# Layer 3's gelu written out over ACT, GpSimd and VectorE, with its down projections two pairs behind

## The chip, the cores and the metric

The kernel runs on one NeuronCore of a Trainium2 chip. The metric is device time in microseconds, the median over executions. Five engines work side by side, each through its own queue of instructions in order: TensorE (PE, with its weight loads shown apart as PEld), VectorE (DVE), ScalarE (ACT), GpSimd (POOL) and SyncE (SP, which issues DMAs here).

## What is computed

Four layers of cross-attention and feed-forward on 2048 tokens of width 256 with a context of 1601 tokens, all in float32, each with a layer norm ahead and a residual. The change is in the last feed-forward block, layer 3, which gives each of eight experts 256 consecutive tokens:

```python
def _L3_ffn_ref(x, w1, b1, w2, b2):
    E = w1.shape[0]                      # 8 experts, width 256, hidden 1024
    tokens = x.reshape(E, T, D)          # T = 256
    h = jnp.einsum('etd,edf->etf', tokens, w1) + b1[:, None, :]
    h = jax.nn.gelu(h)                   # the tanh form
    y = jnp.einsum('etf,efd->etd', h, w2) + b2[:, None, :]
    return y.reshape(B, S, D)
```

The tanh form of gelu is 0.5 h (1 + tanh(0.79788 (h + 0.044715 h^3))).

## The kernel before

Layer 3 is one function, layer3_tail, in which attention and feed-forward are woven together. Tokens come in four chunks of 512 (c = 0 to 3), heads in four groups of four (g), so there are 16 units u = (c, g). Keys come in four tiles of 100 (TK), the part of the context that the mask can close; so the main loop has 64 steps n = (u, kt). The order on TensorE is that of the program text (a manual schedule for PE); on the other engines a scheduler lays the order down when the program is built, and each engine follows it.

One step of the main loop does, in this order: scores of tile kt (L1584, eight matmul records into two psc buffers) and their exponentials on ACT (L1591, two of 100x1024); values of the step before (L1601); maxima of a later unit, first half (L1566 on PE, reduced by VectorE, L1570); one feed-forward bit; the second half of the maxima; a projection of queries (L1551, its two copies qb and q by ACT, L1555 and L1556), or a shift, or a normalisation (L1615, L1617), and, when a chunk is finished, an output projection (L1634); another bit; up to two reciprocals. The psc pool has two buffers, so the maxima of a step wait for its exponentials to have read the scores, and the next scores wait for VectorE's reductions. After a chunk's last head group GpSimd multiplies attention by the reciprocals (L1626).

A bit is one entry of the list that feed_forward(c) makes when the chunk's attention is done; feed(n) runs the next n of them. A chunk has 35 bits: begin (a norm), then for each of its two experts eight steps up, eight steps down and end. With two bits a step, 64 steps do not take all 140, and the experts 5, 6 and 7 are left for the time after the main loop.

- up(e, f, k): two matmuls of 128x256 (L1665) into one half of psu, a PSUM tile of one buffer, then ACT's gelu with the bias b1, from psu into h (L1671). f counts in pairs, k is 0 or 1 within the pair.
- down(e, f, k): two matmuls (L1681) from h and w2 into psy, which sums over all eight.
- end(e): for both token tiles GpSimd adds x and b2 into y (L1691), VectorE adds psy (L1692), SP sends y out (L1693); then the weights of expert e + 2 are loaded (L1531 to L1533). y comes from the pool hp, which has two buffers.

In the list, the steps down of a pair come one pair behind its steps up: up 0, up 1, down 0, up 2, down 1, up 3, down 2, down 3, end.

Of the kernel before, what the change touches and what calls it, by code (L numbers as in the profile page):

```python
# [8 lines left out]
F32 = mybir.dt.float32  # L9
BF16 = mybir.dt.bfloat16  # L10
F32R = mybir.dt.float32r
AF = mybir.ActivationFunctionType
ALU = mybir.AluOpType
AX = mybir.AxisListType

P = 128
D = 256
# [3 lines left out]
CH = 512  # L21
# [32 lines left out]
class Net:  # L54
# [1360 lines left out]
    def layer3_tail(self, mask):  # L1415
        tc, nc, a = self.tc, self.nc, self.a
        H, DH, G = 16, 16, 4
# [4 lines left out]
        with ExitStack() as s:  # L1422
            kv = s.enter_context(tc.tile_pool(name="kv3", bufs=1))
            qp = s.enter_context(tc.tile_pool(name="q3", bufs=3))
            pp = s.enter_context(tc.tile_pool(name="p3", bufs=5))
            op = s.enter_context(tc.tile_pool(name="o3", bufs=2))
# [44 lines left out]
            with ExitStack() as s0:  # L1471
                self.banks(s0)
                for w in (wkT, wqT, wop):
                    nc.gpsimd.memset(w, 0.0)
                nc.gpsimd.memset(v, 0.0)
                nc.gpsimd.memset(v.rearrange("p k (h e) -> p (k h) e", e=32)[:, :, DH : DH + 1], 1.0)
                self.transpose_weight(wkT, raw["Wk"], pad=True)
                self.transpose_weight(wqT, raw["Wq"], pad=True)
                wvT = kv.tile([P, 2, D], F32, name="wvT")
                self.transpose_weight(wvT, raw["Wv"])  # L1480
                nc.vector.tensor_copy(
                    wop.rearrange("p o (h e) -> p (o h) e", e=32)[:, :, 0:DH],
                    raw["Wo"].rearrange("p o (h e) -> p (o h) e", e=DH),
                )
                for g in range(0, G, 2):
                    ps = self.pm()
                    for k in range(2):
                        for o in range(2):
                            nc.tensor.transpose(
                                ps[:, k * D + o * P : k * D + (o + 1) * P],  # L1490
                                wop[:, o, (g + k) * P : (g + k + 1) * P], self.ident,
                            )
                    nc.scalar.copy(woT[:, g : g + 2, :], ps.rearrange("p (k o) -> p k o", k=2))
                for g in range(G):
                    ps = self.pm()
                    for kc in range(2):
                        nc.tensor.matmul(
                            ps[:, :NTAIL], lhsT=wkT[:, kc, g * P : (g + 1) * P], rhs=self.ctxT[:, kc, K0:],
                            start=kc == 0, stop=False,
                        )  # L1500
                    nc.tensor.matmul(ps[:, :NTAIL], lhsT=to17, rhs=away, start=False, stop=True)
                    nc.scalar.activation(kT[:, g, :], ps[:, :NTAIL], AF.Identity, bias=kbias[:, g : g + 1])
                    nc.vector.tensor_copy(kb[:, g, :], kT[:, g, :])
                for kt in range(TK):
                    ps = self.pm()
                    for kc in range(2):
                        nc.tensor.matmul(
                            ps[:TR, :D], lhsT=self.ctxT[:, kc, K0 + kt * TR : K0 + (kt + 1) * TR],
                            rhs=wvT[:, kc, :], start=kc == 0, stop=kc == 1,
                        )  # L1510
                    nc.vector.tensor_tensor(
                        v[:TR, kt, :].rearrange("p (h e) -> p h e", e=32)[:, :, 0:DH],
                        ps[:TR, :D].rearrange("p (h e) -> p h e", e=DH),
                        bv[:TR].rearrange("p (h e) -> p h e", e=DH), ALU.add,
                    )
# [4 lines left out]
            hp = s.enter_context(tc.tile_pool(name="f3h", bufs=2))  # L1520
            E, NF = 8, 8
            b1r = kv.tile([E * NF, P], F32, name="b1r")
            nc.sync.dma_start(b1r, a["L3_ffn_b1"].rearrange("e (f p) -> (e f) p", p=P))
            b1 = kv.tile([P, E * NF], F32, name="b1")
            experts = {}

            def load_expert(e):
                w1 = wp.tile([P, 2, NF * P], F32, name="w1")
                w2 = wp.tile([P, NF, D], F32, name="w2")
                b2 = wp.tile([P, D], F32, name="b2")  # L1530
                nc.sync.dma_start(w1, a["L3_ffn_w1"][e].rearrange("(k p) f -> p k f", p=P))  # L1531
                nc.sync.dma_start(w2, a["L3_ffn_w2"][e].rearrange("(k p) f -> p k f", p=P))
                nc.sync.dma_start(b2, a["L3_ffn_b2"][e].partition_broadcast(P))  # L1533
                experts[e] = w1, w2, b2
# [7 lines left out]
            xnT, q, qb, p_of, acc, attn = {}, {}, {}, {}, {}, {}  # L1542
# [87 lines left out]
            def out_project(c, i):  # L1630
                x = self.x[c * TPC + i]
                ps = self.pm()
                for k in range(G):
                    nc.tensor.matmul(  # L1634
                        ps[:, :D], lhsT=attn[c][:, k, i * P : (i + 1) * P], rhs=woT[:, k, :],
                        start=k == 0, stop=k == G - 1,
                    )
                nc.gpsimd.tensor_tensor(x, x, bo, ALU.add)
                nc.vector.tensor_tensor(x, ps[:, :D], x, ALU.add)
                if i == TPC - 1:  # L1640
                    fbits.extend(feed_forward(c))
# [4 lines left out]
            def feed_forward(c):  # L1646

                state = {}

                def begin():  # L1650
                    if c == 0:
                        ps = self.pm()
                        nc.tensor.transpose(ps[:, : E * NF], b1r, self.ident[: E * NF, : E * NF])
                        nc.vector.tensor_copy(b1, ps[:, : E * NF])
                    state["x"] = self.norm(c)

                def up(e, f, k):
                    w1 = experts[e][0]
                    if k == 0:
                        if f == 0:  # L1660
                            state["h"] = hp.tile([P, NF, 256], F32, name="h3")
                        state["ps"] = psf.tile([P, 2, 256], F32, name="psu", tag="u")
                    ps = state["ps"][:, k, :]
                    for kc in range(2):
                        nc.tensor.matmul(  # L1665
                            ps, lhsT=w1[:, kc, (f + k) * P : (f + k + 1) * P],
                            rhs=state["x"][:, kc, (e % 2) * 256 : (e % 2 + 1) * 256],
                            start=kc == 0, stop=kc == 1,
                        )
                    at = e * NF + f + k  # L1670
                    nc.scalar.activation(  # L1671
                        state["h"][:, f + k, :], ps, AF.Gelu_apprx_tanh, bias=b1[:, at : at + 1]
                    )

                def down(e, f, k):
                    w2 = experts[e][1]
                    if f + k == 0:
                        state["acc"] = psf.tile([P, 2, D], F32, name="psy", tag="y")
                    acc = state["acc"]
                    for i in range(2):  # L1680
                        nc.tensor.matmul(  # L1681
                            acc[:, i, :], lhsT=state["h"][:, f + k, i * P : (i + 1) * P], rhs=w2[:, f + k, :],
                            start=f + k == 0 and i == 0, stop=f + k == NF - 1 and i == 1,
                        )

                def end(e):
                    b2 = experts.pop(e)[2]
                    for i in range(2):
                        t = 2 * e + i
                        y = hp.tile([P, D], F32, name="y")  # L1690
                        nc.gpsimd.tensor_tensor(y, self.x[t], b2, ALU.add)  # L1691
                        nc.vector.tensor_tensor(y, state["acc"][:, i, :], y, ALU.add)  # L1692
                        nc.sync.dma_start(self.out[0, t * P : (t + 1) * P, :], y)  # L1693
                    if e + 2 < E:
                        load_expert(e + 2)

                yield begin, ()
                for e in (2 * c, 2 * c + 1):
                    for f in range(0, NF + 2, 2):
                        for k in range(2):  # L1700
                            if f < NF:
                                yield up, (e, f, k)
                        for k in range(2):
                            if f:
                                yield down, (e, f - 2, k)
                    yield end, (e,)

            def feed(n):
# [17 lines left out]
            for n in range(U * TK):  # L1726
# [12 lines left out]
                elif tasks:  # L1739
                    f, args = tasks.pop(0)  # L1740
                    f(*args)
                if later:
                    f, args = later.pop(0)
# [14 lines left out]
            while later:  # L1758
                f, args = later.pop(0)
# [116 lines left out]
```

## Time and profile before

| | |
|---|---|
| median of three runs | 2328.24 us (2322.44 to 2330.52) |
| the profiled execution | 2327.4 us, span 2325.7 us, mean granted PE clock 0.924 |
| layer 3's attention steps with feed-forward bits | about 1930 to 2245 us |
| experts 5, 6, 7 after the main loop | about 2247 to 2321 us |
| ACT in 1930 to 2245 us, table loads | 51 of 1.283 us |
| GpSimd busy, 1950 to 2000 us | 3.93 us of 50 |

Times are from one execution. A line of the groups gives the source line, engine, operation and tiles, count, busy time and mean duration, then the engine's idle time just before these instructions and what ended it. A line of the waits gives who waited for whom, the total, the number of times and the longest. A line of the timeline gives start, length, engine, source line and operation, and in square brackets the idle time before it and its releaser. TensorE's times are modelled from the instructions' sizes, and a float32 matmul appears as two records. ACT_TABLE_LOAD is the instruction with which ScalarE changes the set of functions that it can evaluate.

### The profile page before, as it was taken

The numbers are of one execution on the slowest core, as the hardware profiler recorded it, in microseconds if no ns is written. First come the engines' busy times: TensorE is split into PE (matmuls) and PEld (weight loads), VectorE is DVE, ScalarE is ACT, GpSimd is POOL, SyncE is SP. The second block draws the span as 40 slices with busy tenths as digits, with TensorE's granted clock in tenths as the row PEclk, the third lists the DMA queues.
The fourth block names the chain that finished last, engine by engine and source line by source line (L and its number), as shares of the span: only waits on it lengthen the run. The fifth ranks groups of instructions, "written<-read, shape, count | busy, mean of one in ns | idle before, by whom it ended". The sixth has DMA issues, their size and how long they took to land.

```text
span 2325.7 us, 22833 instructions
## 1 busy us (share of the span) xinstructions
PE 2006.3 (86%) x8841; PEld 974.4 (42%) x8841; DVE 1208.8 (52%) x2252; ACT 781.0 (34%) x1018; POOL 631.9 (27%) x405
## 2 busy tenths in 40 slices
PE   7799999999986887898978899998877887878887
PEld 3233333333325332344436645555762223333445
DVE  4665555646434999856455532323664453444411
ACT  4544344344440100000224421111433445656441
POOL 1178778778680000000000210000340001000000
PEclk9799999999995999999978999998887788998998
DMA  8810000000000000001010000000002000111111
GB/s 286 269 43 1 1 1 1 1 1 1 1 1 0 1 0 1 0 0 64 0 38 0 21 1 1 0 1 0 1 6 77 1 3 10 34 43 43 43 62 33
DMA packets 39699, 63.51 MB, mean 27 GB/s; under 512 B 5133, under 2 KB 32158, under 8 KB 39582
## 3 DMA queue, kind: packets, MB, share of 16 engines
q1 hardware_dynamic: 37776, 60.33, 8.0%
q10 hardware_dynamic: 1806, 1.64, 0.2%
q8 instruction: 71, 1.16, 0.2%
q14 instruction: 46, 0.38, 0.1%
HBM read 59.87 MB, written 2.10 MB: 27 GB/s over the span
## 4 chain that ended last, share of the span: by engine, by line
PE 65%; DVE 19%; ACT 6%; issue 4%; DMA 3%; POOL 2%; SPq 0%; ACTq 0%; DVEq 0%; POOLq 0%
PE pa L454 6%; PE psc L442 5%; PE psc L627 5%; PE psc L766 4%; PE pa L786 4%; DVE ge L576 4%; PE psc L1584 4%; PE psu L1665 3%; DVE mp L367 3%; PE psy L1681 3%; DVE ge L578 2%; ACT p L1591 2%; DVE ri L404 2%; PE pm L1551 2%; PE pa L1601 1%
## 5 line engine op out<-in xcount | busy, mean ns | idle before, releaser
L463 POOL TENSOR_TENSOR sp<-sp,p 128x1024 f32<-128x1024 f32 (+1 forms) x176 | 418.5, 2378 | 61.6 <-ACT p L447 51.1
L367 DVE TENSOR_REDUCE mp<-pm 128x1 f32<-128x512 f32 x384 | 242.7, 680 | 160.5 <-PE pm L362 159.8
L447 ACT ACTIVATE p<-psc 128x1024 f32<-128x1024 f32 (+1 forms) x208 | 212.9, 1023 | 260.2 <-PE psc L442 169.2
L1570 DVE TENSOR_REDUCE ms<-psc 128x2 bf16<-128x800 f32 x128 | 123.7, 992 | 191.8 <-PE psc L1566 191.8
L442 PE MATMUL psc<-qT,kT 64*128 64x512 f32 (+1 forms) x832 | 221.3, 593 | 0.0
L454 PE MATMUL pa<-p,v 128*64 128x512 f32 (+1 forms) x832 | 202.8, 609 | 0.0
L593 PE MATMUL psc<-ge,pick 128*8 128x512 bf16 x512 | 142.3, 378 | 37.9 <-DVE ge L576 18.9
L1591 ACT ACTIVATE p<-psc 100x1024 f32<-100x1024 f32 x128 | 124.4, 1022 | 94.0 <-PE psc L1584 93.6
L362 PE MATMUL pm<-kb,qb 64*128 64x512 bf16 x384 | 101.8, 393 | 28.0 <-DVE mp L367 26.4
L627 PE MATMUL psc<-w_e,xe 128*128 128x512 f32 x256 | 110.4, 593 | 0.0
L1626 POOL TENSOR_TENSOR attn<-o,ri 128x512 f32<-128x512 f32 x16 | 20.2, 1264 | 328.0 <-DVE ri L1624 306.2
L454 PEld LDWEIGHTS pa<-p,v 128*64 128x64 f32 (+1 forms) x832 | 50.9, 137 | 131.2 <-issue 128.1
L1584 PE MATMUL psc<-q,kT 32*100 32x512 f32 x512 | 96.1, 732 | 10.5 <-DVE ms L1570 10.3
L135 POOL TENSOR_SCALAR rstd<-mv 128x4 f32<-128x4 f32 x32 | 10.5, 328 | 345.0 <-DVE mv L133 345.0
L766 PE MATMUL psc<-q,kT 128*128 128x512 f32 (+1 forms) x208 | 102.2, 610 | 0.0
L576 DVE TENSOR_SCALAR ge<-bc,g 128x128 bf16<-128x128 f32 (+15 forms) x128 | 100.2, 783 | 1.8 <-ACT bc L570 1.8
L829 POOL MEMSET v<- 128x4 f32 x1 | 0.1, 104 | 366.2 <-DVE n_odd L280 366.2
L1665 PE MATMUL psu<-xnT,w 128*128 128x256 f32 x256 | 79.2, 436 | 18.2 <-ACT h L1671 18.2
L442 PEld LDWEIGHTS psc<-qT,kT 64*128 64x128 f32 (+1 forms) x832 | 86.2, 186 | 19.6 <-issue 6.3
L786 PE MATMUL pa<-v,p 128*128 128x257 f32 (+1 forms) x416 | 93.9, 381 | 0.0
L142 DVE TENSOR_SCALAR xn<-x,mv,rstd 128x256 f32<-128x256 f32 x128 | 53.7, 477 | 72.1 <-PE pm L161 63.2
L440 PE MATMUL psc<-sh,negz 64*128 64x512 bf16 (+1 forms) x416 | 87.9, 384 | 3.7 <-ACT sh L389 3.6
(343 smaller groups left out, 3386.3 us busy)
## 6 DMA issues: line engine op xcount, KB each, us to landing
w<-in_L_ffn_w_dram SPq DMA_DIRECT2D x16, 1024.0 KB, 5.6
head<-in_mask_BxSxS_ik_dram SPq DMA_DIRECT2D x16, 600.5 KB, 4.0
head<-in_mask_1x1xSxS_ik_dram SPq DMA_DIRECT2D x16, 600.5 KB, 4.9
tail<-in_mask_BxSxS_ik_dram SPq DMA_DIRECT2D x16, 200.0 KB, 4.2
tail<-in_mask_1x1xSxS_ik_dram SPq DMA_DIRECT2D x16, 200.0 KB, 4.2
x<-in_x_dram SPq DMA_DIRECT2D x16, 128.0 KB, 3.7
w_e<-in_L_ffn_experts_dram SPq DMA_DIRECT2D x2, 1024.0 KB, 7.2
out_dram<-y SPq DMA_DIRECT2D x16, 128.0 KB, 4.9
```

What stands on the lines that cost most here:

```text
L367: nc.vector.tensor_reduce(mp[:, i, j, n : n + 1], pair[j][:, :wd], AX.X, ALU.max)
L442: nc.tensor.matmul(sc[:r, j, :], lhsT=kT[h, hp, kt * P : kt * P + r], rhs=q[h, :], start=False, stop=True,)
L447: nc.scalar.activation(p[:r], sc[:r], AF.Exp, scale=DH**-0.5)
L454: nc.tensor.matmul(acc[h, :], lhsT=v[:r, kt, hp * P + h.start : hp * P + h.stop], rhs=p[:r, j, :], start=kt == 0, stop=kt == NKT - 1,)
L463: nc.gpsimd.tensor_tensor(sums[:r], sums[:r], p[:r], ALU.add)
L576: nc.vector.tensor_scalar(ge[:, :hi], bc[:, :hi], own, None, ALU.is_lt)
L627: nc.tensor.matmul(sc[:, j, :], lhsT=xnT[t // TPC][:, kc, (t % TPC) * P : (t % TPC + 1) * P], rhs=ew[kc][:, half * 4 + 2 * j : half * 4 + ...
L766: nc.tensor.matmul(sc[:r, j, :], lhsT=kT[:, kc, ks], rhs=q[:, kc, :], start=kc == 0, stop=False)
L786: nc.tensor.matmul(acc[:, : D + 1], lhsT=p[:r, kt, i * P : (i + 1) * P], rhs=v[:r, kt, :], start=kt == 0, stop=kt == NKT - 1,)
L1584: nc.tensor.matmul(sc[j // 2][:TR, j % 2, :], lhsT=kT[h, g, kt * TR : (kt + 1) * TR], rhs=q[u][h, :], start=True, stop=True,)
L1591: nc.scalar.activation(p[:TR], sc[k][:TR], AF.Exp, scale=DH**-0.5)
L1665: nc.tensor.matmul(ps, lhsT=w1[:, kc, (f + k) * P : (f + k + 1) * P], rhs=state["x"][:, kc, (e % 2) * 256 : (e % 2 + 1) * 256], start=kc = ...
```

## The change

Four edits, all in layer3_tail.

- Gelu is written out. ACT adds the bias alone (Identity) into h. After both halves of a pair, on 128x512 at a time: GpSimd computes z = h h, z = 0.044715 z + 1, z = z h; ACT takes tanh of 0.79788 z; VectorE writes h = (z + 1) h. The factor 0.5 moves to end, where VectorE's addition becomes 0.5 psy + y. z3 is a new tile in hp, with two buffers.
- The steps down come two pairs behind the steps up: up 0, up 1, up 2, down 0, up 3, down 1, down 2, down 3, end.
- y has one buffer in place of two.
- wvT, the transposed value weights, takes a slice of an attn3 buffer in place of a tile of its own.

```diff
-                wvT = kv.tile([P, 2, D], F32, name="wvT")
+                wvT = op.tile([P, G, CH], F32, name="attn3")[:, 0, :].rearrange("p (k o) -> p k o", k=2)
...
                         state["ps"] = psf.tile([P, 2, 256], F32, name="psu", tag="u")
+                        state["z"] = hp.tile([P, 2, 256], F32, name="z3")
...
-                    nc.scalar.activation(
-                        state["h"][:, f + k, :], ps, AF.Gelu_apprx_tanh, bias=b1[:, at : at + 1]
-                    )
+                    h, z = state["h"][:, f : f + 2, :], state["z"]
+                    nc.scalar.activation(h[:, k, :], ps, AF.Identity, bias=b1[:, at : at + 1])
+                    if k == 1:
+
+                        nc.gpsimd.tensor_tensor(z, h, h, ALU.mult)
+                        nc.gpsimd.tensor_scalar(z, z, 0.044715, 1.0, ALU.mult, ALU.add)
+                        nc.gpsimd.tensor_tensor(z, z, h, ALU.mult)
+                        nc.scalar.activation(z, z, AF.Tanh, scale=0.7978845608028654)
+                        nc.vector.scalar_tensor_tensor(h, z, 1.0, h, ALU.add, ALU.mult)
...
-                        y = hp.tile([P, D], F32, name="y")
+                        y = hp.tile([P, D], F32, name="y", bufs=1)
                         nc.gpsimd.tensor_tensor(y, self.x[t], b2, ALU.add)
-                        nc.vector.tensor_tensor(y, state["acc"][:, i, :], y, ALU.add)
+                        nc.vector.scalar_tensor_tensor(y, state["acc"][:, i, :], 0.5, y, ALU.mult, ALU.add)
...
-                    for f in range(0, NF + 2, 2):
+                    for f in range(0, NF + 4, 2):
                         for k in range(2):
                             if f < NF:
                                 yield up, (e, f, k)
                         for k in range(2):
-                            if f:
-                                yield down, (e, f - 2, k)
+                            if f >= 4:
+                                yield down, (e, f - 4, k)
```

In the changed program as built, tanh stands in ACT's queue between the two exponentials of the step after the pair in experts 0, 3 and 4, and straight after the pair's second bias (in places with a copy between) in experts 1 and 2. In the three experts after the main loop ACT's order is bias three times, tanh 0, bias twice, tanh 1, bias, tanh 2, bias twice, tanh 3. On GpSimd the second y of experts 0 to 3 and 5 and the first y of the next expert stand ahead of that next expert's first chain; around experts 4, 6 and 7 they stand between its chains.

## The prediction

> **What bounds the kernel now.** I read the page's busy shares first, then the waits and groups of layer 3, then two stretches instruction by instruction.
>
> ```profile
> PE 2006.3 (86%) x8841; PEld 974.4 (42%) x8841; DVE 1208.8 (52%) x2252; ACT 781.0 (34%) x1018; POOL 631.9 (27%) x405
> ```
>
> TensorE (PE) carries the kernel. The change touches only the last stage, from 1930 us, in two parts: until 2245 us the feed-forward bits are woven into attention; from 2247 us the last three experts run alone (I number experts 0 to 7; 0 to 4 are woven, 5 to 7 are the tail). The waits of 1930 to 2245 us (who waited for whom: us, times, longest):
>
> ```profile
> PE psc L1566 <- ACT p L1591: 35.5, 33, 2.6
> ...
> POOL y L1691 <- DMA out_dram<-y: 29.4, 3, 19.8
> ...
> PEld psu L1665 <- ACT h L1671: 13.9, 11, 3.5
> ```
>
> TensorE's largest wait there is for the exponentials. The groups of the same stretch hold the loads of activation tables, 51 of 1.283 us, and the rows that I take prices from:
>
> ```profile
> L1671 ACT ACT_TABLE_LOAD x26 | 33.4, 1283 | 0.5
> L1591 ACT ACT_TABLE_LOAD x25 | 32.1, 1283 | 26.6 <-PE psc L1584 26.5
> ...
> L1626 POOL TENSOR_TENSOR attn<-o,ri 128x512 f32<-128x512 f32 x10 | 12.7, 1266 | 222.3 <-DVE ri L1624 222.3
> ...
> L1578 DVE TENSOR_TENSOR q<-pm,q 128x512 f32<-128x512 bf16 x9 | 6.1, 682 | 3.5 <-PE pm L1577 3.5
> ...
> L1617 ACT COPY ri<-pm 128x512 f32<-128x512 f32 x10 | 5.9, 586 | 15.0 <-PE pm L1615 14.7
> ```
>
> What a load costs is seen in two steps of the timeline, ACT's rows and then PE's:
>
> ```profile
> 1988.58 1.94 ACT L1591 ACTIVATE p<-psc 100x1024 f32<-100x1024 f32 x2 [3.21 <-PE psc L1584]
> ...
> 2001.07 1.28 ACT L1591 ACT_TABLE_LOAD   x1 [0.35 <-PE psc L1584]
> 2002.36 1.94 ACT L1591 ACTIVATE p<-psc 100x1024 f32<-100x1024 f32 x2
> ```
>
> ```profile
> 1989.65 0.34 PE L1566 MATMUL psc<-kb,qb 32*128 32x400 bf16 x2 [0.17 <-ACT p L1591]
> ...
> 2003.44 0.34 PE L1566 MATMUL psc<-kb,qb 32*128 32x400 bf16 x2 [1.48 <-ACT p L1591]
> ```
>
> Exponentials without a load keep PE 0.17 us, with one 1.48: the load lies on PE's path whole. The gelu's own load runs after the exponentials, mostly while PE works on.
>
> The tail, PE's rows of expert 7:
>
> ```profile
> 2303.75 1.13 PE L1665 MATMUL psu<-xnT,w 128*128 128x256 f32 x4 [0.62 <-ACT h L1671]
> 2305.45 1.13 PE L1665 MATMUL psu<-xnT,w 128*128 128x256 f32 x4 [0.56 <-ACT h L1671]
> ...
> 2316.68 3.62 PE L1681 MATMUL psy<-w,h 128*128 128x256 f32 x16
> ```
>
> Each step up waits for ACT to have read the step before out of the one psu buffer: spacing 1.70 us. Expert 7 takes from 2302.10 to 2320.30, 18.2 us.
>
> **What the Trainium skill says.** "ScalarE: Activation LUTs", Table sets: exp and tanh lie in one set, gelu elsewhere, identity in every set. The trace agrees for exp and gelu (a load at each change); in the changed program as built one load is left in this stage. Same page, What ACT_TABLE_LOAD costs: 1283 ns and a drain of about 1380. The trace has the 1283, and the exponential 0.01 us behind it (2001.07 + 1.28, 2002.36): no drain, so a load is worth 1.28 and not 2.66. "GPSIMD Engine Reference", Engine selection: two-input elementwise work about half VectorE's rate, one-input work near line rate. The trace: 1.264 us for a two-input 128x512 (L1626), 0.615 for a one-input cast of that size (L672). "Perfetto Trace Analysis", Per-instruction lifecycle: ACT, VectorE and GpSimd are strict FIFO; in this trace ACT's rows stand in program order throughout. So an early tanh holds up every exponential behind it.
>
> **The change part by part.** *New work for each of 32 pairs.* GpSimd: two products and a tensor_scalar. The products 1.264 each; the tensor_scalar is not in the trace at this size: 0.615 as the cast, 1.264 at most as a product. With two gaps of 0.08 (L175 to L176) the chain is 3.30 us, 3.95 above; below, were all three at the cast's price, 2.0. I take 3.30. ACT: Identity for gelu at 0.47 as before, and a tanh of 128x512, between the copy's 0.586 and 0.680 for q with its bias (L1556): 0.65. VectorE: 0.68 as L1578; VectorE waits 123 us for PE in this stretch, which covers it.
>
> *Woven part, 20 pairs.* Removed: 25 loads ahead of exponentials, 25 x 1.28 = 32 us of PE, and of the 13.9 us that steps up waited for gelu some 8 (estimate: about half; the plain 0.47 of the read stays). Added: where tanh stands in ACT's queue. In experts 0, 3 and 4 (12 pairs) it stands between the two exponentials of the next step. With zero at the end of the pair's second step up: bias done 0.54, chain 0.6 to 3.9, tanh 4.0 to 4.65, second exponential 4.65 to 5.6. PE has by then done scores (1.05), values (1.0), first maxima and the next bit, and stands from 3.55 for that exponential until 5.65: 2.1 us, 12 x 2.1 = 25. In experts 1 and 2 (8 pairs) tanh follows the second bias at once. Behind that step up PE has second maxima, mostly 1.9 of projection, a bit and the scores, 2.7 to 4.3 us, before an exponential is wanted; tanh ends at 4.65, and with qb and q (0.69, 0.60) queued behind it in two of the pairs at 5.95. That is 0.35 to 2.0, mean 1.3: 8 x 1.3 = 10.
>
> *y with one buffer.* An expert's second y now waits on GpSimd for the first's output DMA, and the next expert's first y, which stands before that expert's chains, for the second's. After the last step down: VectorE 0.5, issue and landing 5.0, add 0.72, VectorE 0.5, landing 2.0, add 0.72, together 9.5 us (landings of this DMA: 4.9 median, 1.7 least; I take 2.0 for the second, when no weights are in flight). The next chain wants GpSimd at about 7.7 where no norm lies between, in experts 1 and 3: 2 us each, 4. SP's order is output, b2, output, then weights; those land in 5.4 and are wanted tens of us later: nothing. attn on GpSimd can stand behind one chain: hidden by the step until its projection.
>
> Woven sum: -32 - 8 + 25 + 10 + 4 = -1.
>
> *Tail, 12 pairs.* Nothing is left to hide the chain: ACT's queue runs three biases, tanh 0, two biases, tanh 1, one bias, tanh 2, two biases, tanh 3, and step up k+1 waits for bias k. One expert, zero at its first step up:
>
> ```
>         bias done   chain         tanh ends   VectorE ends   down
> pair 0   3.3        3.4 - 6.7      7.45         8.2          10.8 - 12.6
> pair 1   7.9        8.0 - 11.3    12.05        12.8          after up 3
> pair 2  12.5       12.6 - 15.9    16.6         17.3          after down 1
> pair 3  18.8       18.85 - 22.15  22.85        23.6          23.65 - 25.4
> ```
>
> 25.4 against 18.2: 7.2 more. Two pairs of lag don't help, since the last step down of an expert stands before the next one's first step up. Expert 5: four output projections lie between its last downs and hide pair 3; to its first half of down 2 it is 20.9 against 15.4: 5.5. Expert 6 ran its start at about half clock (2.08 for 1.13) and took 23.5; I take 4, between 25.4 (1.9) and 28.3 with the same slow start (4.8). Expert 7: 7.2, and 0.5 for GpSimd held by y. At the end both y were added ahead; now the second follows the first's landing: VectorE 0.5, issue and landing 2.2, add 0.8, VectorE 0.4 = 3.9. Sum 5.5 + 4 + 7.2 + 0.5 + 3.9 = 21.
>
> wvT in attn3's first buffer: written and read before attention starts, nothing.
>
> Sum: +20. The profiled execution took 2327.4 (span 2325.7 and 1.7 around), so 2347.5; the median shown is 0.8 above it: 2348.5, say 2349.
>
> **The rivals.**
> 1. *Faster: the chain is short.* One mechanism: GpSimd does all three at the cast's price, h times h being one stream. At 2.0 us the 12 stalls fall to 0.8 (10 us), the 8 to 0.5 (4), y 2; the tail costs 1.5, 0, 2 and 4.4. Sum -40 + 16 + 8 = -16: 2312. It decides where the chain stays under 2.6 us, by interpolation between the two sums. Against it: all products on GpSimd, of 256, 512 and 1024 elements, have the two-input price (0.72, 1.26, 2.38).
> 2. *Slower: the chain is long.* tensor_scalar at a product's price: 3.95. 20 x 0.65 = 13, and 7 in the tail: 2369. For it: the row is missing. VectorE's new work reads the same memory meanwhile.
> 3. *y holds GpSimd longer.* Both landings at 4.9: held 13 us instead of 9.5; experts 1 and 3 lose 5.6 each and 2 and 4 some 3, 13 more than my 4, and 6 in the tail: 2368. For it: 29.4 us of GpSimd's waits for this DMA now.
> 4. *The clock gives it back.* PE with more pauses is granted a higher clock (by windows of 50 us since 1900 it is 0.83 to 0.97); expert 6 at full clock returns up to 5, a mean 0.05 higher over 315 us of which PE is busy 0.8 some 13: 2331.
> That the loads stay is excluded by the built order.
>
> **How the numbers follow.** Mine (2335 to 2362) 0.50, rival 1 0.14, 2 0.16, 3 0.10, 4 0.10. About 0.3% (7 us) is what a measurement of this kernel can tell from no change. Faster 0.14 is rival 1; same 0.10 is rival 4; slower 0.76 is the rest. The range 2322 to 2378 takes in 2, 3 and 4, and leaves out rival 1 and sums where 2 and 3 add up.
>
> **What would show it.** Right: one table load in the stage; PE's wait for exponentials about as large as its 35.5, now with GpSimd and tanh ahead of it; GpSimd rows of 1.26, 0.6, 1.26; tail experts of about 25 us in the granted full clock; a last y some 4 us after the other. Wrong: PE's wait for exponentials under 15 us, or tail experts under 21 (rival 1); tensor_scalar above 1 us (2); GpSimd waiting over 10 us for each y (3); a clock above 0.97 throughout (4).

## The result, and the profile after

The changed kernel takes 2351.39 us (median; 2347.74 to 2354.0), against 2325.34 for the kernel before on the same chip: ratio 1.0109, 95% interval 1.0083 to 1.0135. It is slower by 26 us there, and by 23 against the median of the time table; +20 was forecast. Its profiled execution took 2351.1 us, span 2349.4, mean granted clock 0.923.

The busy line of the changed kernel's page follows (ACT gave up 48 us, GpSimd took on 95; no table load is left in the woven part, where there were 51):

```profile
PE 2020.8 (86%) x8841; PEld 981.0 (42%) x8841; DVE 1230.6 (52%) x2284; ACT 732.7 (31%) x999; POOL 726.6 (31%) x501
```

Its waits in the woven part (who for whom: us, times, longest):

```profile
ACT z L1679 <- POOL z L1678: 42.8, 20, 4.5
...
POOL y L1698 <- DMA out_dram<-y: 34.8, 5, 14.8
...
PE psc L1566 <- ACT p L1591: 29.3, 36, 3.4
...
PEld psc L1584 <- DVE ms L1570: 14.7, 18, 3.6
...
PEld psu L1666 <- ACT h L1673: 6.5, 9, 3.0
```

TensorE's wait for exponentials is not much shorter than before (29.3 us, and 35.5), and ACT itself now stands 20 times, once a pair, for GpSimd. The fourth line, scores that wait for VectorE's reductions of the maxima, is larger than before (2.7). The groups of the same stretch give the prices of the new work (mean ns after the busy time):

```profile
L1678 POOL TENSOR_TENSOR z<-z,h 128x512 f32<-128x512 f32 x20 | 25.4, 1268 | 1.6
...
L1676 POOL TENSOR_TENSOR z<-h 128x512 f32<-128x512 f32 x20 | 20.8, 1041 | 110.1 <-ACT h L1673 110.1
...
L1680 DVE SCALAR_TENSOR_TENSOR h<-z,h 128x512 f32<-128x512 f32 x20 | 15.0, 750 | 74.0 <-ACT z L1679 74.0
...
L1679 ACT ACTIVATE z<-z 128x512 f32<-128x512 f32 x20 | 12.6, 630 | 42.8 <-POOL z L1678 42.8
L1677 POOL TENSOR_SCALAR z<-z 128x512 f32<-128x512 f32 x20 | 12.4, 621 | 1.7
```

One pair in the timeline, ACT's rows and then TensorE's:

```profile
2217.70 1.02 ACT L1591 ACTIVATE p<-psc 100x1024 f32<-100x1024 f32 x1 [0.63 <-PE psc L1584]
2220.28 0.63 ACT L1679 ACTIVATE z<-z 128x512 f32<-128x512 f32 x1 [1.55 <-POOL z L1678]
2220.82 1.01 ACT L1591 ACTIVATE p<-psc 100x1024 f32<-100x1024 f32 x1
2221.72 0.47 ACT L1673 ACTIVATE h<-psu,b 128x256 f32<-128x256 f32 x1
```

```profile
2218.54 1.13 PE L1666 MATMUL psu<-xnT,w 128*128 128x256 f32 x4
2222.24 2.08 PE L1666 MATMUL psu<-xnT,w 128*128 128x256 f32 x4 [2.57 <-ACT h L1673]
2224.25 2.04 PE L1584 MATMUL psc<-q,kT 32*100 32x512 f32 x8
```

Tanh stands between the two exponentials and waits 1.55 us for GpSimd; the second exponential and the bias behind it wait with it, so TensorE stands 2.57 us. After the pause the same four records take 2.08 us in place of 1.13: it restarts at half clock (.50 granted from 2224 to 2228 us). What half clock adds to the busy time is a term that the sum did not have.

Expert 7 in the tail, TensorE's rows, to be set beside the 1.70 us spacing of before:

```profile
2321.67 1.13 PE L1666 MATMUL psu<-xnT,w 128*128 128x256 f32 x4 [0.56 <-ACT h L1673]
2324.18 1.13 PE L1666 MATMUL psu<-xnT,w 128*128 128x256 f32 x4 [1.38 <-ACT h L1673]
...
2333.54 1.64 PE L1666 MATMUL psu<-xnT,w 128*128 128x256 f32 x4 [3.21 <-ACT h L1673]
2334.98 4.84 PE L1688 MATMUL psy<-w,h 128*128 128x256 f32 x16
2340.31 1.99 PE L1688 MATMUL psy<-w,h 128*128 128x256 f32 x8 [0.50 <-DVE h L1680]
```

The bias that frees psu stands behind a tanh that waits for the chain. The table gives the stages of the profiled executions, cut at the first step up of experts 0, 5, 6 and 7, at the end of the last step down and at the end of the span (us). Busy, idle and clock are TensorE's in the woven part, from the windows of that stretch; idle is length less busy. It holds the same matmuls in all (1286 or 1287 records), so busy times can be compared. The granted clock in the trace is full or half, and "half" adds up the time at half clock in that part. Pauses are idle times of TensorE between matmul rows of at least 1.4 us. Each line is one execution, and that lies up to 6 us from its run's median (e4_nopoly, e7_dvepoly and e6_tailgelu 5 to 6 below).

| kernel | woven | exp. 5 | exp. 6 | exp. 7 | end | busy | idle | clock | half | pauses |
|---|---|---|---|---|---|---|---|---|---|---|
| before | 313.9 | 31.2 | 23.5 | 18.2 | 5.4 | 258.2 | 55.7 | .92 | 51.2 | 22 |
| after | 318.3 | 37.4 | 26.3 | 25.6 | 7.1 | 266.1 | 52.2 | .91 | 54.6 | 16 |
| e1_ident | 254.9 | 31.2 | 22.3 | 18.2 | 5.9 | 235.9 | 19.0 | .99 | 3.4 | 0 |
| e2_lag2 | 315.2 | 32.0 | 26.0 | 19.0 | 4.4 | 260.6 | 54.6 | .91 | 54.6 | 20 |
| e3_y2 | 303.4 | 37.9 | 28.2 | 25.1 | 4.2 | 256.3 | 47.1 | .94 | 37.5 | 16 |
| e4_nopoly | 269.9 | 31.9 | 19.9 | 19.0 | 8.5 | 248.4 | 21.5 | .96 | 23.9 | 2 |
| e5_defer | 280.5 | 41.8 | 31.7 | 29.2 | 6.8 | 251.3 | 29.2 | .96 | 23.9 | 6 |
| e6_tailgelu | 314.7 | 32.6 | 22.4 | 18.2 | 8.6 | 262.2 | 52.5 | .93 | 44.4 | 16 |
| e7_dvepoly | 284.0 | 32.4 | 26.8 | 19.7 | 6.9 | 251.0 | 33.0 | .96 | 20.5 | 5 |
| e8_best | 265.9 | 31.2 | 23.7 | 18.2 | 5.0 | 243.0 | 23.0 | .98 | 10.2 | 3 |
| e9_pad | 280.7 | 31.0 | 19.1 | 18.2 | 5.6 | 238.1 | 42.7 | .99 | 6.8 | 2 |
| e10_lag1 | 312.4 | 37.1 | 29.5 | 28.4 | 7.2 | 260.4 | 52.0 | .93 | 44.4 | 14 |
| e11_best_dve | 278.4 | 31.2 | 22.6 | 18.2 | 5.0 | 252.9 | 25.5 | .95 | 27.3 | 2 |
| e12_pad3 | 282.2 | 31.2 | 22.4 | 18.2 | 5.3 | 248.3 | 33.9 | .95 | 30.7 | 8 |

After less before: woven +4.4, experts +6.2, +2.8 and +7.4, end +1.7, and 1.2 before layer 3's first step up, which is no part of the change: 23.7, the difference of the spans. So the tail and the end make +18, and the woven part gives nothing in return for 25 table loads taken from the exponentials.

The woven part's +4.4 is idle time 3.5 lower and busy time 7.9 higher. The clock is little of the latter: half clock lasts 54.6 us in place of 51.2. TensorE is busy for 50.4 and 48.8 us of that, and if half of it is what half clock adds, 0.8 us (an estimate) comes from the clock. Most of the rest, some 5.5 us (286 records at a mean of 157 ns in place of 137), lies in scores that ran long at full clock. TensorE's rows and weight loads of two steps of the changed kernel, both at a granted clock of 1.00:

```profile
1987.32 1.12 PE L1584 MATMUL psc<-q,kT 32*100 32x512 f32 x8
...
2019.19 1.93 PE L1584 MATMUL psc<-q,kT 32*100 32x512 f32 x8
```

```profile
2019.19 0.25 PEld L1584 LDWEIGHTS psc<-q,kT 32*100 32x100 f32 x4 [0.33 <-DVE ms L1570]
2020.01 0.25 PEld L1584 LDWEIGHTS psc<-q,kT 32*100 32x100 f32 x4 [0.57 <-DVE ms L1570]
```

In the first step both psc buffers are free, and the first records of all four heads start within 0.02 us of each other. In the second step the second buffer comes 0.8 us after the first, held by VectorE's reduction; the heads run two by two, and the eight records take 0.8 us more, which counts as busy. Of the steps whose scores ran at full clock, 7 took 1.6 us and more from the first record to the last, against 1 before (all others took 1.1 to 1.4).

### The profile page after: what moved, and what is told of

Read it like the earlier page. It is cut to its first block, busy times and chain, and to the rows that moved or that the text cites. A ratio compares the mean times of both kernels' runs of the same rounds, so it can differ in the third digit from the quotient of the medians.

```text
span 2349.4 us, 22949 instructions
## 1 busy us (share of the span) xinstructions
PE 2020.8 (86%) x8841; PEld 981.0 (42%) x8841; DVE 1230.6 (52%) x2284; ACT 732.7 (31%) x999; POOL 726.6 (31%) x501
## 5 line engine op out<-in xcount | busy, mean ns | idle before, releaser
L593 PE MATMUL psc<-ge,pick 128*8 128x512 bf16 x512 | 142.3, 378 | 37.9 <-DVE ge L576 19.2
L1584 PE MATMUL psc<-q,kT 32*100 32x512 f32 x512 | 102.0, 722 | 15.8 <-DVE ms L1570 15.2
L1680 DVE SCALAR_TENSOR_TENSOR h<-z,h 128x512 f32<-128x512 f32 x32 | 23.3, 729 | 131.0 <-ACT z L1679 131.0
```

Of the source, the lines that this page charges most:

```text
L593: nc.tensor.matmul(rk[j // 2][0:E, j % 2, :], lhsT=pick[:, e, :], rhs=ge[:, j * CH : (j + 1) * CH], start=first, stop=last,)
L1584: nc.tensor.matmul(sc[j // 2][:TR, j % 2, :], lhsT=kT[h, g, kt * TR : (kt + 1) * TR], rhs=q[u][h, :], start=True, stop=True,)
```

## The experiments

### What the loads are worth: e1_ident

```diff
-                        state["h"][:, f + k, :], ps, AF.Gelu_apprx_tanh, bias=b1[:, at : at + 1]
+                        state["h"][:, f + k, :], ps, AF.Identity, bias=b1[:, at : at + 1]
```

> The kernel before with Identity in place of gelu in layer 3 (gelu itself is left out; nothing else is changed). No exponential of this stage has a table load ahead of it any more, and nothing is added. My theory: the loads ahead of the exponentials lie whole on TensorE's path, so the woven part loses 25 x 1.28 = 32 us and some 8 of the waits of steps up, the tail about 1: 40 us faster than before, ratio 0.983. Rival: the loads are mostly hidden behind TensorE or VectorE, which are the bound: under 12 us faster, ratio over 0.995.

Measured: 2267.59 us, ratio 0.9738 (0.9717 to 0.9758): 60 us faster, where 40 were expected. Idle time fell by 36.7, about what was forecast for loads and waiting gelus together; busy time for the same matmuls fell by another 22.3, as time at half clock went from 51.2 us to 3.4.

### The lag alone: e2_lag2

The kernel before with its gelu kept, and the list of the change:

```diff
-                    for f in range(0, NF + 2, 2):
+                    for f in range(0, NF + 4, 2):
...
-                            if f:
-                                yield down, (e, f - 2, k)
+                            if f >= 4:
+                                yield down, (e, f - 4, k)
```

> The kernel before, its own gelu, with nothing changed but the steps down two pairs behind the steps up. My theory: the lag alone costs little: in the tail a step down fills one pause of TensorE less per expert, 0.6 to 1 us each, and the woven part is the same: 2 to 3 us slower, ratio 1.001. Rival: the drain at the end of every expert, which two pairs of lag lengthen, is what makes the tail slow: some 7 us for each of three experts, 20 slower, ratio 1.009.

Measured: 2329.51 us, ratio 1.001 (1.0001 to 1.002): at most a fifth of a per cent, as the theory had it.

### Two buffers for y: e3_y2

```diff
-            b1r = kv.tile([E * NF, P], F32, name="b1r")
+            b1r = raw["Wv"][: E * NF, 0, :P]
...
-                        y = hp.tile([P, D], F32, name="y", bufs=1)
+                        y = hp.tile([P, D], F32, name="y")
```

(b1r, a small tile of the setup, moves into a free one to make room.)

> The changed kernel with two buffers for y as before, and the rows of b1 put where the raw value weights were, for the space. My theory: one buffer costs 4 us in the woven part and some 2 to 4 at the end: 6 to 8 us faster than the changed kernel, ratio to before about 1.008. Rival: GpSimd held by the output DMAs is the main cost of the change: 19 us or more faster than the changed kernel, ratio to before about 1.002.

Measured: 2334.31 us, ratio 1.0025 (1.0016 to 1.0033): 17 us below the changed kernel, over twice the theory's 6 to 8 and near the rival's 19. In the woven part it is 14.9: idle 5.1, busy 9.8. The place is not the one that the prediction named. VectorE's and then TensorE's rows of the changed kernel where an expert ends:

```profile
1994.30 0.42 DVE L1699 SCALAR_TENSOR_TENSOR y<-psy,y 128x256 f32<-128x256 f32 x1 [3.30 <-POOL y L1698]
1994.64 0.99 DVE L1570 TENSOR_REDUCE ms<-psc 128x2 bf16<-128x800 f32 x1
```

```profile
1995.68 1.66 PE L1584 MATMUL psc<-q,kT 32*100 32x512 f32 x4 [2.73 <-DVE ms L1570]
1997.27 1.94 PE L1601 MATMUL pa<-p,v 100*32 100x512 f32 x8
```

GpSimd waits for the first output to land before it writes the second y. VectorE, which adds psy to that y, waits 3.30 us for GpSimd with a reduction of the maxima queued behind it; the next scores wait for the reduction, 2.73 us, and half clock sets in as they go on (1.94 us for the values, in place of 1.07). With two buffers the wait of scores for reductions falls from 14.7 to 4.7 us.

### Without the polynomial: e4_nopoly

GpSimd's three instructions are gone and tanh reads h; the cubic term is left out.

```diff
-                        nc.gpsimd.tensor_tensor(z, h, h, ALU.mult)
-                        nc.gpsimd.tensor_scalar(z, z, 0.044715, 1.0, ALU.mult, ALU.add)
-                        nc.gpsimd.tensor_tensor(z, z, h, ALU.mult)
-                        nc.scalar.activation(z, z, AF.Tanh, scale=0.7978845608028654)
+                        nc.scalar.activation(z, h, AF.Tanh, scale=0.7978845608028654)
```

> The changed kernel without GpSimd's three instructions for each pair: tanh is taken of h directly (the cubic term of gelu is left out). Everything else stays: tanh on ACT, the product on VectorE, the lag, one buffer for y. My theory: the latency of GpSimd's chain, in front of tanh in ACT's queue, is the cost. Without it a tail expert takes about 19.3 us in place of 25 and the woven part is some 30 us shorter than before: 25 us faster than before, ratio 0.989. Rival: tanh on ACT, the product on VectorE, the lag and y are the cost: it stays near the changed kernel, ratio 1.005 to 1.010.

Measured: 2288.67 us, ratio 0.9837 (0.9816 to 0.9858), 63 us below the changed kernel and 38 below the kernel before, where 25 were expected. Idle time in the woven part falls by 30.7, busy time by 17.7, and the tail by 18.5. The woven part is still 15.0 us longer than e1_ident's, but that is the size of what one buffer for y cost in e3_y2 (14.9), and this run keeps the one buffer. So little is left for the new tanh and product by themselves; what costs is the wait for GpSimd at the head of ACT's queue.

### The order on ACT: e5_defer

The chain stays on GpSimd; tanh and product of a pair are issued after the next step's exponentials. ACT's order is now the text's too.

```diff
-            s.enter_context(tc.manual_schedule(engines={mybir.EngineType.PE}))
+            s.enter_context(tc.manual_schedule(engines={mybir.EngineType.PE, mybir.EngineType.Activation}))
...
-                        nc.scalar.activation(z, z, AF.Tanh, scale=0.7978845608028654)
-                        nc.vector.scalar_tensor_tensor(h, z, 1.0, h, ALU.add, ALU.mult)
+                        ripe.append((h, z))
+                        if not weaving[0]:
+                            finish()
...
+            def finish():
+                while ripe:
+                    h, z = ripe.pop(0)
+                    nc.scalar.activation(z, z, AF.Tanh, scale=0.7978845608028654)
+                    nc.vector.scalar_tensor_tensor(h, z, 1.0, h, ALU.add, ALU.mult)
...
                 scores(u, kt)
+                finish()
```

> The changed kernel with tanh and the product of a woven pair issued after the next step's two exponentials, so that tanh stands behind them in ACT's queue; the tail and the one y buffer are unchanged. Theory (tanh, waiting for GpSimd at the head of ACT's in-order queue, is what holds up the exponentials): PE's idle time in the woven part falls from 52 us to about 25-30, PE's wait for exponentials from 29.3 us to under 12, and the granted clock there rises from .91 to about .95, which takes some 10 us more; 25 to 40 us below the changed kernel, ratio to the kernel before 0.994 to 1.000. Rival (the chain's own length reaches the steps down, or GpSimd is the limit): the wait moves to the steps down waiting for the product, within 5 us of the changed kernel, ratio 1.008 to 1.012.

Measured: 2325.85 us, ratio 0.9995 (0.9986 to 1.0003), 26 below the changed kernel. In the woven part the gain is 37.8: idle 23.0, busy 14.8. Its waits there:

```profile
ACT z L1719 <- POOL z L1678: 11.4, 12, 2.9
...
PE psc L1566 <- ACT p L1591: 4.7, 21, 0.6
```

So the chain, as long as ever, costs TensorE little in the woven part once no exponential stands behind it. The edit also fixes the rest of ACT's order by the text, and no run parts the two in the woven part; the fall of the two waits speaks for the moved tanh. But the tail changed, where the expectation has it unchanged: with ACT's order by the text each tanh stands straight behind its pair's second bias, while the scheduler had put another bias between for most pairs. ACT's rows at the head of expert 5:

```profile
2217.54 0.47 ACT L1673 ACTIVATE h<-psu,b 128x256 f32<-128x256 f32 x1 [1.22 <-PE psu L1666]
2222.08 0.63 ACT L1719 ACTIVATE z<-z 128x512 f32<-128x512 f32 x1 [4.07 <-POOL z L1678]
2222.62 0.46 ACT L1673 ACTIVATE h<-psu,b 128x256 f32<-128x256 f32 x1
```

The three experts took 13.4 us longer than in the changed kernel (4.4, 5.4, 3.6), tanh and the bias behind it waiting as in these rows.

### The tail with one-operation gelu: e6_tailgelu

```diff
+                    if e >= 5:
+                        nc.scalar.activation(h[:, k, :], ps, AF.Gelu_apprx_tanh, bias=b1[:, at : at + 1])
+                        return
...
-                    for f in range(0, NF + 4, 2):
+                    lag = 2 if e >= 5 else 4
+                    for f in range(0, NF + lag, 2):
```

(and the factor in end is 1.0 for these experts, f >= lag and f - lag in the list).

> The changed kernel with the gelu as one operation of ACT and a lag of one pair in experts 5 to 7, where nothing is woven; the rest is the changed kernel's. Theory (the chain uncovered in the tail is a cost by itself): experts 5, 6 and 7 come back to about 31, 24 and 18 us, 16 us below the changed kernel, ratio 1.004; the woven part stays at 318 us within 2. Rival (the shorter pauses in the tail come with another clock, as in the woven part): up to 8 us more or less than that, seen in the length of expert 6 above all.

Measured: 2335.33 us, ratio 1.0035 (1.0022 to 1.0047), 16 below the changed kernel. The three experts return 16.1 (4.8, 3.9, 7.4) and the last is at 18.2 again. The woven part, which the edit leaves alone, was 3.6 shorter in the profiled execution, where 2 were allowed for.

### The polynomial on VectorE: e7_dvepoly

```diff
-                        nc.gpsimd.tensor_tensor(z, h, h, ALU.mult)
-                        nc.gpsimd.tensor_scalar(z, z, 0.044715, 1.0, ALU.mult, ALU.add)
-                        nc.gpsimd.tensor_tensor(z, z, h, ALU.mult)
+                        nc.vector.tensor_tensor(z, h, h, ALU.mult)
+                        nc.vector.tensor_scalar(z, z, 0.044715, 1.0, ALU.mult, ALU.add)
+                        nc.vector.tensor_tensor(z, z, h, ALU.mult)
```

> The changed kernel with the polynomial's three instructions on VectorE in place of GpSimd; order and lag are the same. Theory (the length of the chain sets the cost): the chain falls from about 3.0 us to about 1.9, so PE's idle time in the woven part falls by 20 pairs x 1.0 = 15 to 20 us and each tail expert by 4; 25 us below the changed kernel, ratio 1.000. Rival (VectorE is in PE's way already: its maxima and copies then stand behind 2 us of polynomial): the waits for VectorE's reductions grow from 14.7 us to over 30, and the time stays within 5 us of the changed kernel, ratio 1.009 or more.

Measured: 2305.2 us, ratio 0.9906 (0.989 to 0.9923), 46 below the changed kernel, where 25 were expected. Idle time fell by 19.2, inside the forecast; busy time by another 15.1, which the theory did not have; half clock lasts 20.5 us in place of 54.6. The experts of the tail lost 5.0, nothing (26.8 for 26.3; it starts at half clock, 2.08 for 1.13, up to its first step down) and 5.9. VectorE's groups there:

```profile
L1676 DVE TENSOR_TENSOR z<-h 128x512 f32<-128x512 f32 x20 | 13.5, 674 | 11.9 <-ACT h L1673 11.9
L1678 DVE TENSOR_TENSOR z<-z,h 128x512 f32<-128x512 f32 x20 | 13.5, 673 | 0.4
L1677 DVE TENSOR_SCALAR z<-z 128x512 f32<-128x512 f32 x20 | 8.9, 444 | 0.4
```

The chain is 1.8 us in place of 2.9 (without gaps), and the scores' wait for reductions grew only from 14.7 to 17.6.

### The repairs together: e8_best and e11_best_dve

The edits of e5_defer, e6_tailgelu and e3_y2 in one kernel; then the same with the edit of e7_dvepoly.

> The three repairs together: tanh and product behind the next exponentials, the gelu as one operation of ACT in experts 5 to 7, and two y buffers. If the three costs add (about 30, 16 and 17 us below the changed kernel) less some 10 that the clock gives only once: 2290 to 2300, ratio 0.985 to 0.989. If the clock gains more with each pause taken away: about 2275, ratio 0.978. If the costs overlap, no better than 2325, ratio 1.000.

> The three repairs together and the polynomial on VectorE in place of GpSimd. With tanh behind the exponentials the chain's length should no longer reach TensorE, so a shorter chain gives little, while VectorE's reductions then stand behind 1.7 us more of work for each pair: theory, within 4 us of the version with GpSimd (2275 to 2283, ratio 0.978 to 0.981). Rival (part of the chain still reaches TensorE by the steps down or by y and attn on GpSimd): 8 us or more below it, ratio under 0.975.

Measured: e8_best 2278.99 us, ratio 0.9788 (0.9771 to 0.9804); e11_best_dve 2290.94 us, ratio 0.9847 (0.9826 to 0.9868). The first beats both kernels, the one before by 48 us and the changed one by 72, near the 2275 of its second expectation. Over the changed kernel that is the sum of the parts, 26, 17 and 16, and of the 13 that the tail had lost in e5_defer and doesn't lose here: 72. The second met neither expectation: with VectorE the version is 12 us slower, idle +2.5, busy +9.9, as half clock lasts 27.3 us in place of 10.2. Once tanh is out of the way the shorter chain has nothing left to give, and VectorE's extra work is in the way: the scores' wait for reductions is 13.7 us in place of 5.9.

### Pauses and the clock: e9_pad and e12_pad3

e1_ident, with the first exponential repeated where a step up ran since the last one: once at each of 25 places, or three times at every third of them.

```diff
+                    if k == 0 and ran:
+                        nc.scalar.activation(p[:TR], sc[k][:TR], AF.Exp, scale=DH**-0.5)
+                        ran.clear()
                     nc.scalar.activation(p[:TR], sc[k][:TR], AF.Exp, scale=DH**-0.5)
...
                     at = e * NF + f + k
+                    ran.append(k)
```

The second of the two, against the first:

```diff
                     if k == 0 and ran:
-                        nc.scalar.activation(p[:TR], sc[k][:TR], AF.Exp, scale=DH**-0.5)
                         ran.clear()
+                        count.append(k)
+                        for _ in range(3 if len(count) % 3 == 0 else 0):
+                            nc.scalar.activation(p[:TR], sc[k][:TR], AF.Exp, scale=DH**-0.5)
```

> The kernel before with the bias alone in place of the gelu (which is left out, as in the first experiment), so no table loads, but with the first exponential of a step done twice wherever a step up ran since the last one: 25 more of 0.97 us on ACT, where the 25 loads of 1.28 stood, 24 us. Theory (pauses of TensorE lower its granted clock, wherever they come from): PE's idle time in the woven part goes from 19 us to about 43, and PE's busy time for the same matmuls from 236 us to about 254, the clock from .99 to about .94; the part takes 297 us, the whole 2310, ratio 0.992. Rival (the clock of the first experiment had another cause, such as ACT's loads themselves or what the gelu draws): the idle time grows by 24 and the busy time stays at 236; the part takes 279 us, the whole 2292, ratio 0.984.

> As the run with 25 exponentials done twice, with the same sum in fewer and longer pauses: at every third of those 25 places, 8 in all, the first exponential is done three times more (2.9 us), 24 in all. The gelu is left out as there. Theory (a pause of TensorE is followed by a few us at half clock where it is long, some 1.5 us and more, and is not where it is about 1.2 us): each of the 8 pauses is followed by a stretch at half clock that costs 2 to 3 us, as in the changed kernel; TensorE is idle for about 42 us again, but busy for 252 to 258 us in place of 238, clock about .94; the woven part takes 294 to 300 us in place of 281, ratio to the kernel before about 0.991. Rival (the length of a pause doesn't matter): idle 42, busy 238, clock .99, ratio 0.984 as there. Second rival (much of a pause of 2.9 us is hidden where the first of 0.97 already waits): idle under 35.

Measured: e9_pad 2291.83 us, ratio 0.9843 (0.9815 to 0.9872): idle +23.7, busy +2.2, clock .99. My theory fell for pauses of this length, and the rival's numbers held: 25 short pauses cost their own length and almost nothing else. But neither the loads nor the gelu, the rival's causes, are needed for half clock, since e12_pad3 has neither. e12_pad3 2291.89 us, ratio 0.9859 (0.9838 to 0.988): idle only +14.9 over e1_ident (33.9 us, under the second rival's 35), since part of each longer pause is hidden; but busy +12.4 and clock .95, the theory's effect at a somewhat smaller size. The timeline shows it. TensorE's rows around a pause in e9_pad:

```profile
2094.49 1.06 PE L1606 MATMUL pa<-p,v 100*32 100x512 f32 x8
2096.72 0.34 PE L1566 MATMUL psc<-kb,qb 32*128 32x400 bf16 x2 [1.17 <-ACT p L1596]
2097.00 1.13 PE L1670 MATMUL psu<-xnT,w 128*128 128x256 f32 x4
```

and in e12_pad3:

```profile
2095.87 1.06 PE L1608 MATMUL pa<-p,v 100*32 100x512 f32 x8
2099.02 0.52 PE L1566 MATMUL psc<-kb,qb 32*128 32x400 bf16 x2 [2.08 <-ACT p L1598]
2099.46 2.08 PE L1689 MATMUL psy<-w,h 128*128 128x256 f32 x4
2101.47 0.52 PE L1566 MATMUL psc<-kb,qb 32*128 32x400 bf16 x2
2101.92 2.08 PE L1689 MATMUL psy<-w,h 128*128 128x256 f32 x4
```

The windows of e12_pad3 show the granted clock there (from and to, length, busy times with records in brackets for PE, PEld, DVE, ACT and POOL, clock, DMA share, GB/s):

```profile
2092.00:2096.00 4.00, 4.00 (x28) 2.09 (x31) 3.32 (x5) 1.33 (x3) 1.27 (x1) 1.00 0.28 86
2096.00:2100.00 4.00, 1.92 (x11) 0.72 (x8) 0.43 (x1) 3.94 (x5) 0.00 (x0) 0.87 0.43 176
2100.00:2104.00 4.00, 4.00 (x14) 2.03 (x12) 1.57 (x2) 0.94 (x1) 0.00 (x0) 0.50 0.01 4
2104.00:2108.00 4.00, 3.88 (x21) 1.31 (x22) 0.57 (x1) 2.03 (x3) 0.00 (x0) 0.78 0.00 0
```

Of the eight pauses of 2.0 to 2.5 us six are followed by a stretch at half clock, by such windows of about 3.4 us or twice that (here (0.13 + 0.50 + 0.22) x 4 x 2 = 6.8); seven stretches in the part make the 12.4 us of busy time, about 2 each. The 26 pauses of 1.0 to 1.4 us in e9_pad go with two stretches in all. The Trainium skill, "TensorE: Matmul & The Clock Gate", Part 1: The HAM clock gate, has the clock at half or full by how busy TensorE was in windows of 3413 ns; the lengths agree. As a rule the page gives "no PE-idle gaps >~3.4µs" (HAM oscillation — how this bites in real kernels); here pauses of 2.1 us were enough in most cases, and the measurement decides.

### One pair of lag: e10_lag1

```diff
-                    for f in range(0, NF + 4, 2):
+                    for f in range(0, NF + 2, 2):
...
-                            if f >= 4:
-                                yield down, (e, f - 4, k)
+                            if f:
+                                yield down, (e, f - 2, k)
```

> The changed kernel with the steps down one pair behind the steps up, as before the change; all else is the changed kernel's. Theory (in the woven part a pair's chain ends within the step that follows, so the second pair of lag hides nothing there; in the tail the step down of pair 0 now stands ahead of the third pair's steps up): woven part 318 us within 4, and experts 6 and 7 a pair's wait longer, 3 to 4 us each; 5 to 8 us above the changed kernel, ratio 1.014. Rival (the second pair of lag carries the chain in the woven part): steps down wait there for VectorE's product, 20 pairs by 1 to 2 us, 20 to 40 us above the changed kernel, ratio 1.02 to 1.03.

Measured: 2350.66 us, ratio 1.0102 (1.0081 to 1.0123), the changed kernel's. Neither theory's size: experts 6 and 7 did lose 3.2 and 2.8, as expected, but the woven part won 5.9 (busy 5.7 of it). Steps down waited for the product once in TensorE's matmuls, 1.3 us, and once in its weight loads, 2.2 us, so the second pair of lag hides next to nothing in the woven part. The lower busy time goes with less time at half clock, 44.4 us in place of 54.6; why it is less was not followed up.

## Why the prediction was right, and where its terms were not

The sum of +20 against +23.7 is in part luck: terms that it lacked cancel each other.

- *Loads and waiting gelus, -40.* Right: 36.7 of idle time went with them (e1_ident). Missing beside it: 22.3 us of busy time. The loads made pauses of 1.45 to 1.48 us before TensorE's maxima; the kernel before has 22 pauses of 1.4 us and more and half clock in 12 stretches, against none and 1 in e1_ident. A load was worth more than its 1.28 us.
- *Tanh in ACT's queue, +25 and +10.* Right in mechanism (e4_nopoly, e5_defer) and near in size: without the y term the idle time is 47.1 (e3_y2), 28.1 above e1_ident's where 35 were forecast. The chain was 3.1 us (1.04, 0.62, 1.27 and the gaps), not 3.30. Neither rival 1's chain of 2.0 nor rival 2's of 3.95 came true. Missing again: the busy time, 20.4 above e1_ident's.
- *y with one buffer, +4.* In idle time 5.1, but through VectorE's queue and the reductions, where the step had GpSimd's chains; 9.8 of busy time came on top. With the end it is 17 us (e3_y2), against the 8.4 that the prediction's three terms make. This is rival 3's direction and size by another way; its sign, over 10 us of waiting for each y, did not show (34.8 us in five waits).
- *VectorE's product, covered.* 0.75 us, and by idle time it costs little: e4_nopoly still has it and has 21.5 us, 2.5 above e1_ident's. But what VectorE does later than before can delay a reduction, and that cost shows as busy time of the scores: some 5.5 us in the changed kernel, for which the sum had no term. How much of it is the product's, how much the late exponentials' and y's, was not taken apart.
- *Rival 4, the clock gives it back.* Its premise was that TensorE with more pauses is granted a higher clock. The runs show nothing of it: .99 at 19 us of idle time, .91 to .92 at 52 to 56. And the length of pauses matters, not their sum (e9_pad, at .99 with 43 us, and e12_pad3). The change replaced 22 pauses by 16, but 9 of those are 1.9 us and longer, where the kernel before had 2, and so time at half clock stayed about the same (54.6 us, and 51.2). Here is the luck: what the loads' going gave back at half clock, the pauses for tanh and y took again, and neither was in the sum. With that cancelled, idle time down by 3.5, the longer scores' 5.5 or so and 1.6 of busy time that was not placed leave the woven part at +4.4 in place of -1.
- *The tail.* Forecast 5.5, 4 and 7.7; measured 6.2, 2.8, 7.4, and 4.8, 3.9 and 7.4 come back with the one-operation gelu (e6_tailgelu). The table of bias, chain, tanh and step down held. *The last y, +3.9*: 1.7. The second y came 3.0 us after the first (3.4 by the prediction's terms), but as the last output it travelled alone: from the end of VectorE's last addition to the end of the span it is 3.6 us, against 4.6 before.
- *The lag* gives nothing: e2_lag2 and e10_lag1.

Open: when a pause brings half clock. Of the changed kernel's 30 us of busy time above e1_ident, some 24 are half clock (50.4 us of busy time in it against 3.0, halved) and some 6 the longer scores, both estimates. But e11_best_dve has half clock in six stretches with only two pauses of 1.4 us and more: pauses that are short but close together may count too. That wasn't tried.

## What to carry to other kernels

In these traces an instruction that waited for another engine held up all that stood behind it in its engine's queue: before a step is spread over engines, look at which urgent work will stand behind each hand-over (here tanh before an exponential, y before a reduction), and issue the late half after it. Price a pause of TensorE by its length: about 1.2 us cost itself here, and 2 us often cost as much again at half clock. Look at long rows too: a wait for one buffer of two can show as busy time. Where nothing is woven in, one operation of 0.47 us with a single table load beat the chain of bias, three steps on GpSimd, tanh and product (e6_tailgelu).

## What was not expected of the hardware

- A product of a tensor with itself took 1.04 us on GpSimd (128x512), one of two tensors 1.27; with VectorE's product running beside it in the tail the first took 1.18.
- VectorE's (z + 1) h took 0.69 us alone in the tail and 0.75 in the mean of the woven part; in e8_best, beside GpSimd's chains, 0.83.
- On VectorE, which was expected to be in the way, the three steps of the polynomial took 0.67, 0.44 and 0.67 us, 1.8 against GpSimd's 2.9 without gaps.
- Scores of four heads whose two psc buffers came free together took 1.12 us for eight records. Where the second buffer came later, at the same full clock, they took 1.93 (after, 2019.19 us).
